# First Wq loads on ScalarE's queue, finished rows on SyncE's or ScalarE's, and a new order of all operations

## The chip, the cores and the metric

The kernel runs on one core of a Trainium2 chip. The metric is the device time of one execution in microseconds (us). The engines are TensorE (PE), VectorE (DVE), ScalarE (ACT), GpSimd (POOL) and SyncE (SP). PE multiplies into PSUM, DVE, ACT and POOL do the elementwise work, and SP issues most transfers. Each engine carries out its own instructions strictly in order and waits, where it has to, on semaphores that the others raise.

## The reference, cut to what matters

A cross-attention layer in fp32: batch 2, 2048 tokens, width 640, 8 heads of 80; the context has 128 tokens, of which the last 4 (`ca`) belong to an adapter.

```python
query = x @ Wq;  keyt = enc @ Wk;  valt = enc @ Wv        # enc: 124 text tokens
hs    = mha(query, keyt, valt)                            # text attention
ca_q1 = einsum('btc,th->bch', ca, Wq_ca)[:, indices, :]   # 384 rows, each repeated for 2048 positions
ca_hs1 = mha(ca_q1, x, x)                                 # adapter, first attention: over all tokens
ca_hs2 = mha(ca_hs1 @ Wq, ca @ Wk_ca, ca @ Wv_ca)         # adapter, second attention: 4 keys
out = (hs + ca_hs2) @ Wout + b_out + x
```

## The kernel before, in words

All text work goes through 16 units of 256 tokens, 8 for each of the two samples. For each unit PE makes queries (`pq`, out of transposed rows `xt` and `wq_sb`), scores against the text keys (`sc`), attention outputs (`ph`, out of transposed probabilities `pT`) and the output projection (`po`). Queries and projection are products with fewer multiplications: sums and differences of blocks go in (`x_sums`, `wq_sums`, `wout_sums`, and for each `ph` a set of sums in `hs`), partial products go through PSUM and are added by DVE (`q`, and the two buffers of output rows, `x_more` and `last_rows`). A row tile starts as a load of x, gathers its projections by adds on DVE and the adapter's part by an accumulating indirect transfer of POOL (`add_second`: `x_more<-o,query` or `last_rows<-o,query`), and is stored to `out_dram`.

The adapter runs beside it, sample by sample. Its first scores are made twice. The first time (`s<-zop,cop`) DVE only takes their maxima (`mx`, 128 x 2048 elements at a time, 24 for each sample); the second time ACT takes exponentials (`ea`, again 24 for each sample), and PE sums them against `y_sb` into `acc`. A tile of first scores gets its bank of PSUM only when DVE has read the one before it. From `acc` a short chain (`prod`, `s2f`, `p`, then the transpose `pt_p` on PE, `p2T`, `po`, `o`) makes the second attention's result `o`, which `add_second` gathers from DRAM.

The order of everything is written out by hand, or rather by a search whose result is a table. Coroutines give operations (`Do`: engine or engines, function, what it waits for). The class `Desk` (L64) has a table `TURNS` (L85 to L292) with a number for each operation. `Desk.run` takes the operation with the lowest number, and the number modulo six names the engine. So the table alone sets each engine's order and, where a `Do` names several engines, which of them does the work. `Desk.dma` (L445) puts a transfer on ACT's queue when the table gave it to ACT, otherwise on SP's; its times (`us`, `issue`, `more`) are only the search's idea of a transfer, and don't reach the program. Transfers of both queues share eight completion semaphores, in turn: a transfer waits at its issue until the one eight places ahead of it, on either queue, has landed.

At the start, 14 `unread` products of zeros keep PE busy ahead of and between its first real work, and `first_loads` (L667) loads four row tiles of x (`xz`) and Wq (`wq_sb`) in five pieces, all on SP in the order x0, Wq0, x1, Wq1, Wq2, Wq3, the five strips of Wq4, x2, x3, `wqca`, the context, and two more weights. `residual` (L2329) loads rows, `stored` (L2507) stores them: POOL accumulates, then SP stores. The last unit's rows go out in halves (`stored_half`, L2498), on SP or ACT.

Of the kernel before, what the change touches and what calls it, by code (L numbers as in the profile page):

```python
# [14 lines left out]
P = 128  # L15
# [50 lines left out]
class Desk:  # L66
# [393 lines left out]
def kernel(  # L460
# [206 lines left out]
    def first_loads():  # L667

        def whole(at):
            t = xrow.tile([P, 4 * H], F32, tag="xz", name="xz")  # L670
            rows_of[0] = t.rearrange("p (k n) -> p k n", k=4)

        yield Do("NONE", whole, [], needs=[(staging, 1)])

        def x_rows(k):
# [26 lines left out]
        for c in (2, 3):  # L702
            yield chunk(c)
# [1887 lines left out]
```

## Time and profile before

| | us |
|---|---|
| Median of 3 runs (573.73, 575.43, 575.57) | 575.43 |
| The profiled execution, its own time | 576.6 |
| Its span, first to last instruction | 574.9 |
| PE busy | 564.9 (98%) |
| DVE busy | 399.1 (69%) |
| ACT busy | 285.4 (50%) |
| POOL busy | 167.3 (29%) |
| Mean granted TensorE clock | 0.996 |

The profiled execution lies 1.2 us above the median and 1.7 us of it lie outside the span. PE is busy for all but 10 us of the span, so a new order can win little more than those: 1.1 us ahead of PE's first instruction, some 3.3 us behind its last, and short waits between. The engines' shares are means over stages with different limits. In one stage DVE takes the maxima and is itself busy without a gap; in another ACT takes the exponentials; in the last 75 us only PE has much to do, and POOL and the transfers of rows run beside it. What a wait costs has to be read in its stage.

### The profile page before, as it was taken

The page shows a single profiled execution, that of the slowest core. Times are in us where ns is not written, and L with a number is a line of the kernel's source. Part 1 is how long each engine was busy: PE and PEld are TensorE (multiplying, and loading weights), DVE is VectorE, ACT ScalarE, POOL GpSimd, SP SyncE. Part 2 cuts the span into 40 slices and gives each one's busy share as a digit, 9 for nine tenths or more (in the row PEclk, how much of TensorE's full clock was granted, in tenths as well). Part 3 has the DMA queues.
Part 4 walks back from the last instruction along what each step waited for, and adds up shares of the span by engine and source line. Part 5 has one row for each costly group of instructions (what it writes and reads, how often), then busy time and mean ns, then how long its engine had stood idle before and what let it go on. Part 6 is the DMA issues. An engine that isn't in the chain of part 4 may idle for free.

```text
span 574.9 us, 18865 instructions
## 1 busy us (share of the span) xinstructions
PE 564.9 (98%) x8069; PEld 307.9 (54%) x8069; DVE 399.1 (69%) x657; ACT 285.4 (50%) x808; POOL 167.3 (29%) x220
## 2 busy tenths in 40 slices
PE   9999999999999999999989999999999999999987
PEld 8885334555556455465545454555545545455543
DVE  2475999999998656567999999996422332645353
ACT  1113255476656799899845556534646664000000
POOL 8202023310622062103114342521412141155162
PEclk9999999999999999999989999999999999999999
DMA  7998485876878867536725989886564496889978
GB/s 221 219 245 137 142 174 156 158 203 146 199 193 192 233 161 185 163 122 188 249 65 166 315 247 324 210 268 227 140 207 93 138 271 196 247 201 240 261 132 244
DMA packets 145690, 113.20 MB, mean 197 GB/s; under 512 B 82548, under 2 KB 116980, under 8 KB 145608
## 3 DMA queue, kind: packets, MB, share of 16 engines
q1 hardware_dynamic: 139688, 101.00, 61.1%
q0 software_dynamic: 5632, 10.69, 10.8%
q8 instruction: 63, 1.03, 0.7%
q10 hardware_dynamic: 288, 0.33, 0.2%
q14 instruction: 19, 0.16, 0.1%
HBM read 71.60 MB, written 40.39 MB: 195 GB/s over the span
## 4 chain that ended last, share of the span: by engine, by line
PE 85%; DVE 6%; DMA 4%; ACT 4%; issue 1%; POOL 0%; SPq 0%; ACTq 0%; POOLq 0%
PE po L405 24%; PE pq L405 21%; PE acc L396 7%; PE sc L396 7%; PE s L396 6%; PE ph L396 6%; PE pq L396 4%; PE pyz L396 2%; DVE mx L427 2%; ACT ea L427 2%; DMA out_dram<-x_more 2%; DMA last_rows<-o,query 1%; PE pv L396 1%; PE pk L396 1%; ACT p L427 1%
## 5 line engine op out<-in xcount | busy, mean ns | idle before, releaser
L427 ACT ACTIVATE p<-sc,m 128x124 f32<-128x124 f32 x256 | 90.1, 379 | 42.8 <-DVE m L427 42.8
L427 DVE TENSOR_REDUCE mx<-s 128x4 f32<-128x2048 f32 x48 | 109.2, 2275 | 1.3 <-PE s L396 1.2
L427 ACT ACTIVATE ea<-s 128x2048 f32<-128x2048 f32 x48 | 90.7, 1890 | 35.9 <-PE s L396 35.8
L427 POOL TENSOR_TENSOR p<-p,r 128x992 f32<-128x992 f32 x16 | 30.2, 1891 | 176.9 <-DVE r L427 175.4
L405 PE MATMUL po<-wout_sums,hs 128*32 128x320 f32 x1024 | 78.4, 434 | 1.6 <-POOL hs L427 1.6
L405 PE MATMUL po<-wout_sb,hs 128*32 128x320 f32 x928 | 71.5, 433 | 0.1
L405 PE MATMUL pq<-xt,wq_sb 128*32 128x256 f32 (+1 forms) x928 | 66.6, 422 | 0.0
L427 DVE TENSOR_TENSOR x_more<-x_more,po 128x320 f32<-128x320 f32 x68 | 32.3, 480 | 43.4 <-PE po L405 42.9
L427 DVE TENSOR_TENSOR last_rows<-last_rows,po 128x320 f32<-128x320 f32 x60 | 28.4, 482 | 41.4 <-PE po L405 41.2
L427 ACT ACTIVATION_READ_ACCUMULATOR p<-sc,m 128x1 f32 x256 | 56.6, 221 | 0.0
L427 POOL TENSOR_TENSOR hs<-hs 128x256 f32<-128x256 f32 x35 | 32.5, 953 | 63.6 <-DVE hs L427 56.3
L405 PEld LDWEIGHTS po<-wout_sums,hs 128*32 128x32 f32 x1024 | 31.7, 110 | 35.8 <-issue 3.2
L396 PE MATMUL acc<-ea,y_sb 128*32 128x384 f32 (+2 forms) x768 | 50.2, 383 | 0.4 <-ACT ea L427 0.4
L396 PE MATMUL ph<-pT,vpad 128*32 128x256 f32 x768 | 47.5, 380 | 0.0
L427 DVE TENSOR_REDUCE m<-sc 128x4 f32<-128x496 f32 x64 | 40.5, 659 | 9.1 <-PE sc L396 9.0
L2350 POOL DMA_INDIRECT x_more<-o,query x17 | 26.7, 1571 | 64.6 <-DVE x_more L427 34.5
L405 PEld LDWEIGHTS po<-wout_sb,hs 128*32 128x32 f32 x928 | 29.3, 110 | 30.1 <-issue 1.2
L405 PEld LDWEIGHTS pq<-xt,wq_sb 128*32 128x32 f32 x928 | 28.3, 111 | 28.9 <-issue 14.6
L427 DVE STREAM_TRANSPOSE eb<-p 128x1024 f32<-128x1024 f32 x32 | 39.4, 1233 | 2.5 <-DMA kept<-eb 1.4
L396 PEld LDWEIGHTS sc<-kmain,q 64*128 64x128 f32 x512 | 31.5, 187 | 12.2 <-issue 6.1
L396 PE MATMUL sc<-kmain,q 64*128 64x124 f32 x512 | 37.6, 284 | 0.0
L405 PE MATMUL pq<-xt,wq 128*32 128x512 f32 x280 | 34.1, 595 | 0.0
(219 smaller groups left out, 823.3 us busy)
## 6 DMA issues: line engine op xcount, KB each, us to landing
kept<-eb SPq DMA_DIRECT2D x32, 512.0 KB, 4.2
pT<-kept SPq DMA_DIRECT2D x16, 1024.0 KB, 7.6
landing<-away SPq DMA_DIRECT2D x15, 512.0 KB, 4.7
xi<-in_x_dram SPq DMA_DIRECT2D x56, 128.0 KB, 4.0
x_more<-in_x_dram SPq DMA_DIRECT2D x17, 320.0 KB, 4.5
out_dram<-x_more SPq DMA_DIRECT2D x16, 320.0 KB, 5.1
last_rows<-in_x_dram SPq DMA_DIRECT2D x15, 320.0 KB, 6.5
out_dram<-last_rows SPq DMA_DIRECT2D x14, 320.0 KB, 3.7
```

Of the source, the lines that this page charges most:

```text
L396: self.pin(self.nc.tensor.matmul(out, lhsT, rhs, **kw))
L405: self.pin(self.nc.tensor.matmul(out[j : j + 32], lhsT[:, j : j + 32], rhs, **kw))
L427: self.pin(getattr(engine, what)(*args, **kw))
L2350: desk.pin(nc.gpsimd.indirect_dma_start(out=t, out_offset=None, in_=o2_of[b], in_offset=bass.IndirectOffsetOnAxis(ap=query[:, st : st + 1] ...
```

## The change

Three things. The loads of Wq become a task of their own on ACT's queue, so that SP issues the four row tiles one behind the other. `stored` may use SP or ACT, and the table chooses: in the changed program 14 finished row tiles or halves are stored by ACT, where before only the last two halves were. And the whole table is new; it was searched with other numbers for how long transfers take (the third arguments and `more` of the calls of `dma`), which themselves leave the program as it is. PE's work is the same in both programs: 4494 products, the 14 of zeros among them.

```diff
     TURNS = {
-        ".1": [791], ".2": [38, 53, 54, 72, 84, 96, 102, 114, 126, 156, 168, 180, 192, 198, 234, 762], ".3": [536],
+        ".1": [1025], ".2": [44, 59, 60, 84, 96, 108, 114, 120, 126, 132, 150, 174, 198, 210, 234, 1002], ".3":
...
+        def of_wq():
+
+            for c in range(4):
+                yield chunk(c)
+            yield Do("ACT", last, [], marks=[("wq", 4)])
+
...
-            return Do("SP", go, [], marks=[("wq", c)])
+            return Do("ACT", go, [], marks=[("wq", c)])
...
-        for k in (0, 1):
-            yield x_rows(k)
-            yield chunk(k)
-        for c in (2, 3):
-            yield chunk(c)
-        yield Do("SP", last, [], marks=[("wq", 4)])
-        for k in (2, 3):
+        yield Fork(of_wq(), 0)
+        for k in range(4):
             yield x_rows(k)
...
-            "SP", lambda: dma(pT.rearrange("p i k h a -> p i (k h a)"), by_keys, 2.85, 0.42, 2.6),
+            "SP", lambda: dma(pT.rearrange("p i k h a -> p i (k h a)"), by_keys, 3.6, 0.42, 1.9),
...
-        yield Do("SP", lambda: dma(rows_out, t, 0.8, 0.37), frees=[(rows, i)])
+        yield Do(("SP", "ACT"), lambda: dma(rows_out, t, 1.15, 0.37, 1.45), frees=[(rows, i)])
...
-        desk.free[e] = 0.8
+        desk.free[e] = 0.85 if e == "ACT" else 0.8
```

The places that the prediction speaks of follow, as each engine's order stands in the two programs. The numbers behind names are those of buffers.

DVE at the second attention of sample 0, before: `m`, `p` and `r` are its small softmax, `mx` the maxima of the first scores of sample 1, `eb` and `q` belong to the text units.

```order
L427 TENSOR_REDUCE m_0_3849<-s2f 128x24
L427 TENSOR_TENSOR p_0_3705<-s2f,m_0_3849 128x96
L427 TENSOR_REDUCE mx_3252<-s_1_0_1_0_3838 128x4
L427 STREAM_TRANSPOSE eb_1_3899<-p_831 128x1024
L427 TENSOR_REDUCE r_0_3706<-p_0_3705 128x24
L427 RECIPROCAL r_0_3706<-r_0_3706 128x24
L427 TENSOR_TENSOR p_0_3705<-p_0_3705,r_0_3706 128x96
L427 TENSOR_TENSOR q_3752<-q_3752,pq_1_3855 128x2x256
L427 TENSOR_TENSOR q_3752<-q_3752,pq_0_3753 128x2x256
```

The same place after.

```order
L427 TENSOR_REDUCE m_0_3833<-s2f 128x24
L427 TENSOR_TENSOR p_0_3699<-s2f,m_0_3833 128x96
L427 RECIPROCAL r_3_3722<-r_3_3722 128x8
L427 TENSOR_REDUCE mx_3167<-s_1_0_1_0_3836 128x4
L427 SCALAR_TENSOR_TENSOR zop_3_3585<-zop_3_3585,low_z,zb_3_0_3724 128x512
L427 STREAM_TRANSPOSE eb_1_3897<-p_830 128x1024
L427 TENSOR_REDUCE r_0_3700<-p_0_3699 128x24
L427 RECIPROCAL r_0_3700<-r_0_3700 128x24
L427 TENSOR_TENSOR p_0_3699<-p_0_3699,r_0_3700 128x96
L427 TENSOR_TENSOR q_3752<-q_3752,pq_0_3753 128x2x256
L427 TENSOR_TENSOR q_3752<-q_3752,pq_1_3861 128x2x256
```

The combination of `zop`, which before stood ahead of `prod`, `s2f` and `m`, now stands behind the maxima, and the two adds into `q` have changed places. In both programs the transpose `pt_p` on PE waits for the add that reads `pq_1`.

POOL in the last 75 us, before: `hs` are sums of a unit's attention outputs, the DMAs accumulate the adapter's rows.

```order
L427 TENSOR_TENSOR hs_5056<-hs_5056 128x256
L2350 DMA last_rows<-o_1_6406,query 128x640
L427 TENSOR_TENSOR hs_4223<-hs_4223 128x256
L2350 DMA x_more<-o_1_6406,query 128x640 x2
L2350 DMA last_rows<-o_1_6406,query 128x640
L427 TENSOR_TENSOR hs_5056<-hs_5056 128x256
L2350 DMA x_more<-o_1_6406,query 128x640
L427 TENSOR_TENSOR hs_4130<-hs_4130 128x256
L2350 DMA x_more<-o_1_6406,query 128x640 x2
L2350 DMA last_rows<-o_1_6406,query 128x640 x3
```

The same after.

```order
L427 TENSOR_TENSOR hs_5064<-hs_5064 128x256
L2351 DMA last_rows<-o_1_6388,query 128x640
L2351 DMA x_more<-o_1_6388,query 128x640
L427 TENSOR_TENSOR hs_5064<-hs_5064 128x256 x2
L2351 DMA x_more<-o_1_6388,query 128x640 x4
L2351 DMA last_rows<-o_1_6388,query 128x640
L427 TENSOR_TENSOR hs_5064<-hs_5064 128x256
L2351 DMA x_more<-o_1_6388,query 128x640
L2351 DMA last_rows<-o_1_6388,query 128x640 x3
```

Before, the third `hs` sum here is the first of the four sums of its unit that the projection needs. After, that sum is DVE's, made right behind its copy of `ph`; POOL's last `hs` sum is the one that the projection needs last.

ACT among the exponentials of sample 1, after; before, this stretch of ACT held the same exponentials and copies and no DMA.

```order
L427 ACTIVATE ea_1_7_6082<-s_1_1_7_6073 128x2048
L427 COPY hs_5064<-ph_2_6094 128x512
L447 DMA out_dram<-last_rows 128x640
L427 ACTIVATE ea_1_8_6124<-s_1_1_8_6115 128x2048
L447 DMA out_dram<-x_more 128x640
L447 DMA out_dram<-last_rows 128x640
L427 COPY wout_sums<-ph_4_6125 128x256
L427 ACTIVATE ea_1_9_6178<-s_1_1_9_6169 128x2048
L427 ACTIVATE ea_1_10_6213<-s_1_1_10_6204 128x2048
```

SP's last transfers, before; the last two half rows of all are ACT's.

```order
L447 DMA out_dram<-x_more 128x640 x2
L447 DMA out_dram<-last_rows 128x320
L447 DMA out_dram<-last_rows 128x640
L447 DMA out_dram<-x_more 128x640
L447 DMA out_dram<-last_rows 128x640
L447 DMA out_dram<-last_rows 128x320
L447 DMA out_dram<-last_rows 128x640
```

SP's last transfers after; ACT stores the first half of the very last row, SP the second, and a whole row behind it.

```order
L447 DMA out_dram<-x_more 128x640
L447 DMA last_rows<-in_x_dram 128x640
L447 DMA x_more<-in_x_dram 128x640
L447 DMA out_dram<-x_more 128x640
L447 DMA out_dram<-last_rows 128x640 x2
L447 DMA out_dram<-x_more 128x320 x2
L447 DMA out_dram<-last_rows 128x640
```

More of the change, by code (lines that the diff above doesn't have):

```diff
@@ L676, in x_rows @@
             return Do(
-                "SP", lambda: dma(rows_of[0][:, k], x[0, k * P : (k + 1) * P, :], (0.3, 0.9, 1.65, 1.65)[k], more=2.3),
+                "SP", lambda: dma(rows_of[0][:, k], x[0, k * P : (k + 1) * P, :], (0.45, 0.9, 1.2, 1.2)[k], more=2.3),
                 [], marks=[("xrows", k)],
@@ L685, in go @@
                 if c < 2:
-                    dma(wq_sb[:, c, :], pair, 1.65, more=2.3)
+                    dma(wq_sb[:, c, :], pair, (0.45, 1.0)[c], more=2.3)
                 else:
@@ L1360, in of_pairs @@
                 d1 = VR + (R * i + VH) % P
-                dma(most[part, :2], v[:, 0::2, :, d0 : d0 + R], 2.16, 1.31)
+                dma(most[part, :2], v[:, 0::2, :, d0 : d0 + R], 1.7, 1.31)
                 desk.pin(nc.sync.dma_start(most[part, 2:], v[:, 1::2, :, d1 : d1 + R]))
@@ L1708, in part_away @@
             def part_away(i, k=k, z=z):
-                dma(away[k, :, i].rearrange("q (g n) -> q g n", g=4), z[:, i].bitcast(F32), 0.31, 0.45)
+                dma(away[k, :, i].rearrange("q (g n) -> q g n", g=4), z[:, i].bitcast(F32), 0.48, 0.45, 1.6)
             op = yield Do("ACT", lambda: desk.a_copy(z[:, 0], pq[:, cols]), [at], rank=0)
@@ L1797, in yz_block @@
                 yield Do(
-                    "SP", lambda u=u: dma(away[:, u], zs, 0.65, 0.38), frees=[(zss, i)],
+                    "SP", lambda u=u: dma(away[:, u], zs, 0.3, 0.38, 1.8), frees=[(zss, i)],
                     marks=[("zop", b, sb, u, "away")],
@@ L1811, in back @@
                     zs = cap.tile([P, 512], F32, tag=f"zs{z[0]}", name=f"zb_{b}_{sb}_{u}")
-                    dma(zs, away[:, u], 1.2, 0.38)
+                    dma(zs, away[:, u], 1.15, 0.38, 1.4)
                     return zs
@@ L1847, in away @@
             def away(t=op.value, u=u):
-                dma(kept[:, :, u, :], t.rearrange("p (a n) -> p a n", a=4), 0.85, 0.53)
+                dma(kept[:, :, u, :], t.rearrange("p (a n) -> p a n", a=4), 0.9, 0.53, 1.6)
             yield Do("SP", away, frees=[(yts, op.slots[0][0])], marks=[("y out", b, sb, u)], rank=0.5)
@@ L1862, in back @@
                     y_sb[R * a : R * (a + 1), sb].rearrange("p g u s k -> p g (u s k)"),
-                    by_tokens[a], 0.59, 0.38,
+                    by_tokens[a], 0.67, 0.38, 1.7,
                 )
@@ L2108, in second @@
                 yield Fork(one(Do(
-                    "SP", lambda ct=ct: dma(o2_of[b][ct * P : (ct + 1) * P, :], o2[:, ct], 1.2, 0.37),
+                    "SP", lambda ct=ct: dma(o2_of[b][ct * P : (ct + 1) * P, :], o2[:, ct], 0.9, 0.37, 1.75),
                     [("o2 part", b, ct)], marks=[("o2 out", b, ct)],
@@ L2335, in load @@
                 t = row_of[at[0]]
-                dma(t, x[b, st * P : (st + 1) * P, :], 0.95, 0.37)
+                dma(t, x[b, st * P : (st + 1) * P, :], 1.06, 0.37, 1.85)
                 return t
```

410 rows, old and new, of the table TURNS are left out of this document.

## The prediction

> **What bounds the kernel now.** I read the busy shares of the page first, then all that PE waited for, then a table of stages, and then the instructions at each wait.
>
> ```profile
> PE 564.9 (98%) x8069; PEld 307.9 (54%) x8069; DVE 399.1 (69%) x657; ACT 285.4 (50%) x808; POOL 167.3 (29%) x220
> ```
>
> PE is the bound: of a span of 574.9 us it is idle for 10.0. Its waits, grouped by what ended them (total, times, longest, in us):
>
> ```profile
> PE s L396 <- DVE mx L427: 2.1, 4, 1.1
> PE po L405 <- POOL hs L427: 1.6, 1, 1.6
> PE unread L396 <- DVE zeros L427: 1.1, 1, 1.1
> PE s L396 <- ACT ea L427: 0.6, 3, 0.2
> PE pt_p L396 <- DVE q L427: 0.5, 1, 0.5
> PE acc L396 <- ACT ea L427: 0.4, 2, 0.2
> ```
>
> Two places hold most of what an order can change: the maxima with the second attention's `pt_p` (2.1 + 0.5), and one `po` that waits for POOL (1.6). The stages (from:to, length; busy of PE, PEld, DVE, ACT, POOL; granted clock; share of the DMA engines; GB/s):
>
> ```profile
> 7.17:20.00 12.83, 12.81 (x77) 11.54 (x77) 5.64 (x19) 2.31 (x6) 9.49 (x18) 1.00 0.89 274
> 290.00:300.00 10.00, 8.26 (x116) 4.61 (x108) 9.24 (x12) 3.15 (x12) 0.00 (x0) 0.83 0.25 79
> 293.90:297.30 3.40, 2.97 (x36) 1.57 (x40) 3.40 (x4) 0.60 (x2) 0.00 (x0) 0.50 0.73 231
> 300.00:390.00 90.00, 88.99 (x1280) 46.51 (x1280) 87.03 (x103) 48.13 (x199) 34.45 (x31) 1.00 0.84 254
> 440.00:500.00 60.00, 60.00 (x946) 29.61 (x942) 22.72 (x53) 28.41 (x22) 12.68 (x11) 1.00 0.67 196
> 545.00:556.00 11.00, 9.41 (x144) 4.42 (x140) 6.44 (x14) 0.86 (x2) 7.04 (x6) 1.00 0.62 132
> ```
>
> From 7 us on, PE lacks nothing at the start (12.81 of 12.83). Around 290 us DVE is the bound, 9.24 of 10.00, and stays near it to 390 (87.03 of 90). There the clock is granted at half for 3.40 us, which costs 1.7 us of PE's work beside the waits. Both programs give PE the same products, so the sum is made of waits, the clock, the start and the tail.
>
> **The start.** Moved: Wq's eleven loads go from SP to ACT, two ahead of ACT's table load, the rest between and behind its first three copies of transposes. Before, ten of them held SP:
>
> ```profile
> 2.19 8.24 SPq L447 DMA_DIRECT2D wq_sb<-in_L_xattn_Wq_dram  x10
> 1.13:7.17 6.04, 6.04 (x28) 5.79 (x28) 1.62 (x6) 0.96 (x1) 5.66 (x34) 1.00 0.85 259
> ```
>
> SP was through with them at 10.43, and x2 and x3 came only then. Now the x rows come early, and PE turns row 2 before Wq's second chunk. But PE already had cover for the late rows: it is busy for 6.04 of 6.04 us from its first instruction to 7.17, then for 12.81 of 12.83, and the 14 products of zeros stay. So there is nothing to win, and I put the term at 0. The last strips of Wq now wait on ACT for rows and context to land; PE needs them some 6 us later than SP's last issue of them before, and that cover would have to be used up first. The other end is a loss of 1.0, a little more than the 8.24 / 10 that one of these loads took SP.
>
> **Sample 0's second attention, and the maxima of sample 1.**
>
> ```profile
> 283.84 0.74 DVE L427 SCALAR_TENSOR_TENSOR zop<-zop,low_z,zb 128x512 fp32r<-128x512 f32 x1
> 289.38 2.28 DVE L427 TENSOR_REDUCE mx<-s 128x4 f32<-128x2048 f32 x1
> 293.49 1.28 DVE L427 TENSOR_TENSOR q<-q,pq 128x512 f32<-128x512 f32 x2
> 316.52 0.82 DVE L427 TENSOR_TENSOR wout_sums<-wout_sb 128x640 f32<-128x640 f32 x1
> 291.71 0.51 PE L396 MATMUL s<-zop,cop 32*128 32x512 f32 x4 [1.12 <-DVE mx L427]
> 294.22 1.08 PE L396 MATMUL pt_p<-ident,p 128*32 128x128 f32 x16 [0.52 <-DVE q L427]
> 316.66 0.51 PE L396 MATMUL s<-zop,cop 32*128 32x512 f32 x4 [0.40 <-DVE mx L427]
> ```
>
> `zop` (0.74, some 0.70 net, since neighbours overlap) now follows the maxima at 289.38 instead of preceding them. So the first wait falls from 1.12 to 0.42. But everything DVE does up to `pt_p`'s release is still done, `zop` included, so `pt_p` is released no earlier, and PE stands there 0.70 longer. Worse, `pt_p` waits for the add that reads `pq_1`. It was the first of the pair at 293.49; now it is the second, 1.28 / 2 = 0.64 later. The two waits make 0.42 + (0.52 + 0.70 + 0.64) = 2.28 against 1.64: a loss of 0.64. Further on, one more subtraction, `wout_sums` (0.82), which followed the maxima that end at 316.6, stands ahead of them, and the next `s` is held by that much, less an overlap: up to 0.75. If the two add up, the loss is 1.39, if the second hides in the first, 0.64. I take 1.0. The best end is a gain of 1.1, the 1.12 gone and nothing in its place; the worst, 1.9, adds one more wait like the 0.52, since between 300 and 390 DVE has only 3 us of idle time to give.
>
> **The wait on POOL at 550.9.** The chain of waits, then POOL and PE:
>
> ```profile
> 524.61 7.70 DMA last_rows<-o,query
> 534.41 8.89 DMA out_dram<-x_more
> 543.31 4.92 DMA x_more<-in_x_dram
> 548.34 1.55 POOL L2350 DMA_INDIRECT last_rows<-o,query  x1 [5.67 <-DMA x_more<-in_x_dram]
> 549.33 1.56 POOL L427 TENSOR_TENSOR hs<-hs 128x256 f32<-128x256 f32 x1
> 550.94 1.28 PE L405 MATMUL po<-wout_sums,hs 128*32 128x320 f32 x16 [1.59 <-POOL hs L427]
> ```
>
> SP waits for an accumulate to land before it may store, then for the store to land before it may load the next row; POOL waits for that row; behind it in POOL's order stands the `hs` sum that PE needs. The new order gives this sum to DVE, and POOL's last `hs` sum is used some 8 us of PE's work later. So this wait goes whatever the stores do: -1.59. What is late next is DVE's pair of sums of the same unit, which end close before their use; I leave 0.2 for it. Net -1.4, between -1.6 and 0 (POOL's new place as late as the old).
>
> [...]
>
> **The tail.** Rows of the last 55 us (KB each, median us from issue to landing), and the last issue:
>
> ```profile
> out_dram<-last_rows SPq DMA_DIRECT2D x6, 320.0 KB, 3.6
> out_dram<-x_more ACTq DMA_DIRECT2D x2, 160.0 KB, 1.9
> last_rows<-o,query POOLq DMA_INDIRECT x6, 6.7
> 571.65 0.88 ACTq L447 DMA_DIRECT2D out_dram<-x_more  x2
> ```
>
> Before, a half row on ACT is last. Now SP issues a half when the last add is done and a whole row behind it. That adds one issue, 0.88 / 2 = 0.4, and between nothing and 3.6 - 1.9 = 1.7 for the longer landing. At the very end little else is in flight, so I take 0.4 of this: +0.8, between 0.4 and 2.1.
>
> **The other moves cost nothing** that I can place. The twelve stores that ACT gains besides the two cost it 12 x 0.44 = 5.3 us of issue; it is idle for half of the span (285.4 busy). The `pT` loads keep their places ahead of `ph`.
>
> **The sum**, against the profiled execution's 576.6: 0 + 1.0 - 1.4 + 0.8 = +0.4, so 577.0. That execution lies 1.2 above the median of 575.43, so I say 575.8.
>
> **The rivals.**
>
> Faster: the half clock doesn't come back. It stands at 293.9 to 297.3, behind the waits of 1.12 and 0.52; yet the 1.59 at 550.9 left the clock at 1.00 (545 to 556), so how a wait falls decides, not its length alone. In the new order one wait is short and one long. If the clock stays full and the waits shrink by what I let them grow: 575.8 - 1.7 - 1.0 = 573.1. Against it: the same 2 us of waiting lie in the same 4 us. [...]
>
> Slower: a store on ACT stands ahead of exponentials and waits for its accumulate.
>
> ```profile
> L427 ACT ACTIVATE ea<-s 128x2048 f32<-128x2048 f32 x48 | 90.7, 1890 | 35.9 <-PE s L396 35.8
> SPq L447 <- DMA x_more<-o,query: 41.5, 6, 16.0
> SPq L447 <- DMA last_rows<-o,query: 40.8, 5, 17.4
> ```
>
> On SP such stores waited 82.3 us in 11 times from 440 us on, harmlessly. On ACT, `ea` stands behind, PE's `acc` behind that. An exponential has 35.9 / 48 = 0.75 us of idle time ahead of it, so a store that waits longer delays PE. By the durations of PE's instructions, the closest store among the exponentials stands 6.1 us behind its accumulate, the next 6.7, and an accumulate takes 1.55 on POOL and up to 6.7 to land: waits of 2.2 and 1.6, less 0.75 each, 2.3, and 0.5 for the transfers that then wait for their semaphore's turn. 575.8 + 2.8 = 578.6. Against it: in 440 to 500 PE never waited (60.00 of 60.00), ACT being busy for 28.41, so PE takes the exponentials late.
>
> The move of Wq's loads doesn't do what it says: the strips come late by the 1.0 above, 575.8 + 1.0 = 576.8.
>
> **Chances.** The forecast 0.40 (574.5 to 577.5 by its own terms), the faster rival 0.27, the slower 0.28, the last 0.05. A measurement here tells about 0.3%, 1.7 us, from no change. Faster is the first rival and an edge of the forecast, 0.28; the same is most of the forecast and of the last, 0.38; slower is the second rival with the upper edge, 0.34. The range, 572.2 to 579.0, takes in both rivals' middles.
>
> **What would show it.** Right: no `po` waiting for POOL; `pt_p` waiting near 1.9 us for `q`; a wait at `s` near 316; a whole `last_rows` store landing last, some 3.5 us behind PE's end. Wrong: `acc` waiting for `ea` by more than 0.4 in all, stores on ACT with waits above 0.75 ahead of `ea`, a clock of 1.00 through 290 to 300, or PE idle between 7 and 20 us.

## The result

The changed kernel takes 573.27 us (median of 17 runs, 572.9 to 574.38). The kernel before, run beside it, takes 575.96 us (17 runs, 573.73 to 580.09). The ratio is 0.994, with a 95% interval from 0.992 to 0.996: faster by about 0.6%. The forecast was 575.8, within 0.3% of no change, in a range from 572.2 to 579.0. The time lies in the range, but on the side that had a chance of 0.28.

The runs of the changed kernel lie within 1.5 us of each other, those of the kernel before spread over 6. The profiled execution of the changed kernel took 572.92 us, with a span of 570.9; against the 576.6 and 574.9 of the one before that is 3.7 to 4.0 us, more than the medians' 2.7, because the profiled execution before was slower than its median (by 0.64) and the one after faster (by 0.35). The time falls by 0.3 less than the span: every run of the changed kernel has 2.0 to 2.1 us outside the span, every run of the kernel before 1.7 to 1.8. The prediction had no term for this, and no trace here shows what it is.

### The profile page after: what moved, and what is told of

Read it like the earlier page. It is cut to its first block, busy times and chain, and to the rows that moved or that the text cites. A ratio compares the mean times of both kernels' runs of the same rounds, so it can differ in the third digit from the quotient of the medians.

```text
span 570.9 us, 18875 instructions
## 1 busy us (share of the span) xinstructions
PE 563.0 (99%) x8069; PEld 309.6 (54%) x8069; DVE 394.5 (69%) x659; ACT 287.1 (50%) x806; POOL 160.1 (28%) x213
## 4 chain that ended last, share of the span: by engine, by line
PE 93%; ACT 3%; DVE 3%; DMA 1%; issue 0%; SPq 0%; ACTq 0%
PE po L405 28%; PE pq L405 24%; PE sc L396 8%; PE acc L396 7%; PE ph L396 7%; PE s L396 7%; PE pq L396 4%; PE pyz L396 2%; ACT ea L427 2%; PE pv L396 1%; DVE mx L427 1%; PE pk L396 1%; DMA xz<-in_x_dram 1%; ACT p L427 1%; PE pt_wq L410 1%; PE pw L396 0%
## 5 line engine op out<-in xcount | busy, mean ns | idle before, releaser
L427 POOL TENSOR_TENSOR p<-p,r 128x992 f32<-128x992 f32 x17 | 31.4, 1849 | 130.9 <-DVE r L427 130.9
L405 PEld LDWEIGHTS po<-wout_sums,hs 128*32 128x32 f32 x1024 | 33.4, 110 | 32.7 <-issue 2.7
L427 ACT COPY hs<-ph 128x512 f32<-128x512 f32 (+1 forms) x25 | 13.4, 552 | 57.7 <-PE ph L396 57.7
L427 POOL TENSOR_TENSOR hs<-hs 128x256 f32<-128x256 f32 x31 | 28.9, 1020 | 33.7 <-ACT hs L427 25.4
```

The lines of the kernel that those rows point to most:

```text
L405: self.pin(self.nc.tensor.matmul(out[j : j + 32], lhsT[:, j : j + 32], rhs, **kw))
L427: self.pin(getattr(engine, what)(*args, **kw))
```

## The profile after, beside the one before

The page of the changed kernel, PE's busy time and its waits (total, times, longest):

```profile
PE 563.0 (99%) x8069; PEld 309.6 (54%) x8069; DVE 394.5 (69%) x659; ACT 287.1 (50%) x806; POOL 160.1 (28%) x213
...
PE unread L396 <- DVE zeros L427: 1.1, 1, 1.1
PE s L396 <- DVE mx L427: 1.1, 2, 0.7
PE s L396 <- ACT ea L427: 0.6, 3, 0.2
PE pt_x L410 <- DVE first_rows L427: 0.4, 1, 0.4
PE pt_x L410 <- POOL band_z L541: 0.2, 1, 0.2
PE acc L396 <- ACT ea L427: 0.2, 1, 0.2
```

The wait of 1.6 for POOL's `hs` is gone, and so is that of `pt_p` for `q`. The waits at the maxima are halved. DVE's busy time fell by 4.6 us and POOL's by 7.2.

The stages that answer to the prediction's (from:to, length; busy of PE, PEld, DVE, ACT, POOL; granted clock; share of the DMA engines; GB/s):

```profile
7.17:20.00 12.83, 12.45 (x71) 11.13 (x70) 7.05 (x27) 1.22 (x3) 8.96 (x18) 1.00 0.94 192
290.00:300.00 10.00, 10.00 (x152) 5.87 (x144) 9.93 (x11) 6.94 (x26) 0.00 (x0) 1.00 0.58 196
...
545.00:556.00 11.00, 11.00 (x169) 6.42 (x164) 5.18 (x13) 0.00 (x0) 6.96 (x5) 1.00 0.84 170
```

Between 290 and 300 PE is now busy for all 10.00 us at full clock, where before it was 8.26 at a clock of 0.83.

How far PE is ahead is read from products that both programs have in like number. PE's groups by tile, with the starts of the first and the last product, before:

```profile
L396 PE MATMUL sc<-kmain,q x512: 272/272/371, 71.3 to 389.2; 64*128 64x124 f32 x171
L405 PE MATMUL po<-wout_sums,hs x1024: 429/432/458, 320.2 to 570.1; 128*32 128x320 f32 x171
```

and after:

```profile
L396 PE MATMUL sc<-kmain,q x512: 272/272/371, 71.0 to 385.8; 64*128 64x124 f32 x171
L405 PE MATMUL po<-wout_sums,hs x1024: 429/432/457, 320.1 to 565.2; 128*32 128x320 f32 x171
```

That splits the 4.0 us between the spans by the prediction's terms:

| stretch | forecast | by the traces | read from |
|---|---|---|---|
| start, to the first `sc` | 0 | -0.3 | 71.3 to 71.0 |
| to the last `sc`, with the second attention and the maxima | +1.0 | -3.1 | 389.2 to 385.8, less 0.3 |
| to the last `po`, with the wait on POOL | -1.4 | -1.5 | 570.1 to 565.2, less 3.4 |
| the tail | +0.8 | +0.9 | the spans, less 4.9 |
| sum | +0.4 | -4.0 | |

Three terms came within 0.3. The second is 4.1 off and carries the whole gain. At that place DVE's and POOL's instructions in the timeline of the kernel before (start, us, what):

```profile
284.68 2.28 DVE L427 TENSOR_TENSOR prod<-prod 128x288 f32<-128x288 f32 x2
...
284.84 1.95 POOL L427 TENSOR_TENSOR p<-p,r 128x992 f32<-128x992 f32 x1 [14.97 <-DVE r L427]
...
286.75 1.34 POOL L427 TENSOR_TENSOR x_sums<-xt,x_sums 128x512 f32<-128x512 f32 x1
286.99 1.20 DVE L427 TENSOR_TENSOR s2f<-prod 128x72 f32<-128x72 f32 x1
288.06 1.28 POOL L427 TENSOR_TENSOR x_sums<-xt 128x512 f32<-128x512 f32 x1
...
288.22 0.25 DVE L427 TENSOR_REDUCE m<-s2f 128x24 f32<-128x96 f32 x1
...
288.51 0.95 DVE L427 TENSOR_TENSOR p<-s2f,m 128x96 f32<-128x96 f32 x1
```

and the same DVE instructions after, one by one (shape, busy, mean ns):

```profile
L427 DVE TENSOR_TENSOR prod<-prod 128x144 f32<-128x144 f32 x1 | 0.3, 307 | 0.0
L427 DVE TENSOR_TENSOR p<-s2f,m 128x96 f32<-128x96 f32 x1 | 0.3, 259 | 0.0
L427 DVE TENSOR_REDUCE m<-s2f 128x24 f32<-128x96 f32 x1 | 0.3, 253 | 0.0
L427 DVE TENSOR_TENSOR s2f<-prod 128x72 f32<-128x72 f32 x1 | 0.2, 234 | 0.0
```

Before, the pair of `prod` took 2.28 us, `s2f` 1.20 and `p` 0.95; now 0.76, 0.23 and 0.26, together 3.18 us less, on the same shapes. Before, each of the three ended 0.1 to 0.2 us behind one of POOL's additions and multiplications: 286.96 behind 286.79, 288.19 behind 288.09, 289.46 behind 289.34. The reduction `m`, which reads one operand, took 0.25 in both, beside POOL's 288.06 as well. In the new order none of these POOL instructions stands there: the multiplication of `p` by `r` is ACT's, and of the two `x_sums` one is DVE's and one POOL's, the latter over at 277.6, 6 us ahead of the chain.

## The experiments

The theory after the result was P, for POOL: a DVE instruction with two operands in SBUF is held until a POOL instruction that is under way has ended (the three above end 0.10 to 0.17 us behind POOL's), which before held DVE back by 3.2 us just ahead of the maxima that PE waits for. The rival was O, for order: the gain comes from `zop` behind the maxima, from the other moves of DVE or from the late part. In each edit a number of the table moves one operation, or gives it to another engine (its remainder by six). A line with a minus sign gives the number that stood in the table.

**Before, with POOL's three instructions behind DVE's chain.** POOL's first one waits for a reciprocal of DVE, which here stands behind `p` instead of ahead of `prod`. No engine's work changes.

```diff
-Desk.TURNS[".66.2.2"][6] = 7502
+Desk.TURNS[".66.2.2"][6] = 7538
```

> The kernel before, with one reciprocal of VectorE (0.14 us) moved behind the second attention's chain, so that GpSimd's multiplication and two sums behind it start only after the chain. Theory P (VectorE's elementwise operations with two inputs in SBUF wait for GpSimd's, so prod, s2f and p took 4.4 us instead of 1.3): prod 0.8 for the pair, s2f 0.23, p 0.26, no wait at s near 291 nor at pt_p, no half clock there, 3 to 3.5 us faster than before where that clock was halved, at least 1.6 anyway. Theory O (the gain came from zop standing behind the maxima): prod, s2f and p as long as before, waits 1.1 and 0.5 as before, 0 to 0.3 us.

Measured: 573.35 us (13 runs, 571.71 to 580.07); ratio 0.9932, interval 0.9901 to 0.9962. One reciprocal moved makes the median of the kernel before as low as that of the changed one, though its runs spread over 8.4 us. From the timeline of DVE and POOL:

```profile
284.66 0.76 DVE L427 TENSOR_TENSOR prod<-prod 128x288 f32<-128x288 f32 x2
285.45 0.23 DVE L427 TENSOR_TENSOR s2f<-prod 128x72 f32<-128x72 f32 x1
...
286.00 0.26 DVE L427 TENSOR_TENSOR p<-s2f,m 128x96 f32<-128x96 f32 x1
...
286.52 1.84 POOL L427 TENSOR_TENSOR p<-p,r 128x992 f32<-128x992 f32 x1 [16.61 <-ACT p L427]
...
289.58 1.28 POOL L427 TENSOR_TENSOR x_sums<-xt 128x512 f32<-128x512 f32 x1
...
290.19 0.78 DVE L427 TENSOR_TENSOR p<-p,r 128x96 f32<-128x96 f32 x1
```

The three are short as in the changed kernel. The next one of the kind, the second multiplication of `p`, now meets POOL's last one: 0.78 instead of 0.26, and it ends at 290.97, 0.1 behind POOL's 290.86. That this happens again at another place, with another instruction, speaks for P and leaves next to nothing for O. PE waits neither at `s` near 291 nor at `pt_p`, as expected, but a wait of 0.51 for the maxima is left at a `po` at 294.52. The profiled execution was the slowest of the 13, with a wait of 4.4 us for POOL's `hs` near 551, of which more below.

**Before, with the `hs` sum on DVE.** The one sum that PE waits for at 550.9.

```diff
-Desk.TURNS[".64.3.4"][0] = 13221
+Desk.TURNS[".64.3.4"][0] = 13220
```

> The kernel before, with one hs sum of the last unit but one given to VectorE instead of GpSimd, nothing else. If the wait of 1.59 us near 551 hangs on this sum standing behind an accumulate in GpSimd's order, it goes and the kernel is 1.4 to 1.6 us faster. Rival (the stores on ScalarE's queue are what ends it): another po or ph waits for rows or transfers there, gain below 0.5 us.

Measured: 576.34 us (12 runs, 575.11 to 578.91); ratio 0.9995, interval 0.9966 to 1.0023. The wait is gone, the time is not measurably less; the expected gain of 1.4 to 1.6 isn't seen, though the interval alone, which reaches to 2.0 us, would not exclude it. The trace says where the time went. Stages of this kernel:

```profile
563.00:567.00 4.00, 4.00 (x64) 1.95 (x60) 1.45 (x3) 0.00 (x0) 0.84 (x1) 1.00 1.06 250
567.00:571.00 4.00, 2.69 (x40) 1.04 (x32) 1.48 (x4) 0.00 (x0) 0.00 (x0) 1.00 1.05 342
571.00:575.00 4.00, 0.00 (x0) 0.00 (x0) 0.00 (x0) 0.00 (x0) 0.00 (x0) 0.97 0.53 199
```

PE's last product ends at 569.69, 1.9 earlier than before, but the span ends at 575.0: the tail is 5.3 us, where before it was 3.3. The DMA engines are busy throughout (1.06 and 1.05 of the stretch) and still moving rows when PE is done. In the kernel before, the last two of these stretches read:

```profile
567.00:571.00 4.00, 4.00 (x68) 1.93 (x60) 1.29 (x3) 0.00 (x0) 0.00 (x0) 1.00 0.99 334
571.00:575.00 4.00, 0.61 (x12) 0.02 (x3) 0.97 (x2) 0.00 (x0) 0.00 (x0) 0.85 0.54 201
```

The transfers end when they ended before (0.53 and 0.54 of the last 4 us). So in this order the wait at 551 covered the transfers, and taking it away alone hands its time to the tail. In the same trace the waits near 291 stand as before (1.12 and 0.52), but the clock stayed full there, and instead a third wait of 1.22 came at 296.6. The half clock and that wait are two faces of one lateness of DVE: from the start of the late `s` to the start of the first `po` behind it PE took 5.41 us in the trace with the half clock (291.71 to 297.12), and 5.40 here without it (291.21 to 296.61).

**Both edits together.**

> The kernel before with both edits. If the two waits are all that matters, it reaches the changed kernel's time: 3.0 to 5.0 us faster than before, within 1 us of 573.3, and its times spread as little as the changed kernel's (under 2 us). If the start, the stores on ScalarE or the rest of the new order carry a share, it stays 1 to 2 us above 573.3.

Measured: 573.43 us (12 runs, 571.96 to 578.37); ratio 0.9939, interval 0.9906 to 0.9972: what the first edit gives, and no more. Here too the tail is 5.3 us. The other half of the expectation failed: the runs spread over 6.4 us, where I had expected under 2.

**The changed kernel, with those POOL instructions as before.** The multiplication of `p` goes from ACT to POOL, one `x_sums` from DVE to POOL, and these, the reciprocal ahead of them and POOL's own `x_sums` stand at before's places; everything else stays new.

```diff
-Desk.TURNS[".66.2.2"][6] = 7454
-Desk.TURNS[".66.2.2"][7] = 7609
-Desk.TURNS[".54.4"][0] = 7293
-Desk.TURNS[".54.3"][0] = 7148
+Desk.TURNS[".66.2.2"][6] = 7502
+Desk.TURNS[".66.2.2"][7] = 7539
+Desk.TURNS[".54.4"][0] = 7593
+Desk.TURNS[".54.3"][0] = 7629
```

> The changed kernel with GpSimd's multiplication and two sums put back beside the second attention's chain, as they stood before. Theory P: prod, s2f and p take 4 to 4.5 us again, s and pt_p wait 1.5 to 2.5 us together, and the half clock may come back: 1.5 to 4 us slower than the changed kernel, 574.8 to 577.3. Theory O: prod, s2f and p stay at 1.3 us and the time within 0.5 us of 573.3.

Measured: 577.0 us (12 runs, 576.54 to 577.48); ratio 0.9992, interval 0.9962 to 1.0022. The whole gain is gone. DVE's groups, then the stage, PE's scores by tile, and PE's waits in the timeline:

```profile
L427 DVE TENSOR_TENSOR prod<-prod 128x144 f32<-128x144 f32 x1 | 1.8, 1833 | 0.0
L427 DVE TENSOR_TENSOR s2f<-prod 128x72 f32<-128x72 f32 x1 | 1.2, 1195 | 0.0
L427 DVE TENSOR_TENSOR p<-s2f,m 128x96 f32<-128x96 f32 x1 | 0.9, 945 | 0.0
```

```profile
290.00:300.00 10.00, 8.24 (x104) 4.73 (x100) 9.31 (x14) 4.54 (x15) 0.00 (x0) 0.83 0.30 93
```

```profile
L396 PE MATMUL sc<-kmain,q x512: 272/272/371, 71.0 to 389.6; 64*128 64x124 f32 x171
```

```profile
290.67 0.51 PE L396 MATMUL s<-zop,cop 32*128 32x512 f32 x4 [0.46 <-DVE mx L427]
...
294.44 1.08 PE L396 MATMUL pt_p<-ident,p 128*32 128x128 f32 x16 [1.28 <-DVE q L427]
```

The long instructions are back, to within 5 ns of before's, the last `sc` comes 3.8 later than in the changed kernel, and the waits have the shape that I had forecast: a short one at `s` (0.46; I had 0.42), a longer one at `pt_p` (1.28; I had 1.86), and the half clock. The second is shorter than forecast because PE took 0.50 us more for the scores between them (2.49 against 1.99 before). From the moment PE was free for this `s` to the start of `pt_p` it took 4.23 us, and 3.63 before: 0.60 more, where I had 0.64. My reading of the order of DVE was right for a kernel in which POOL is still there.

**The changed kernel, all stores of finished rows on SP.** Twelve of the fourteen stores that ACT issued go back to SP; the last two halves were ACT's before, too. One line of the twelve:

```diff
+Desk.TURNS[".58.3.10"][2] = 10096
...
```

> The changed kernel with all twelve of its stores of finished rows that had gone to ACT's queue back on SP's, in before's manner; everything else stays. Theory P (the whole gain lies in the stretch 286 to 300, where POOL no longer holds DVE up, and the wait at 551 went because its sum is on DVE): within 0.5 us of the changed kernel's 573.3, no `po` waiting for POOL's `hs`, PE busy 11.00 of 11.00 in 541 to 552; SP waits longer for the accumulates. Theory S (the stores on ACT are what makes the late part smooth): a wait of PE for POOL or for a last sum comes back past 500, 574.5 to 576, and the runs spread as before's do.

Measured: 573.36 us (8 runs, 573.23 to 574.39); ratio 0.9942, interval 0.9919 to 0.9964: the changed kernel's time. PE waits for no POOL sum there, and waits 0.3 us less in all. The queue of the stores is worth nothing here: 573.36 against 573.27.

**The changed kernel, the first loads of Wq on SP.** Four chunks and the five strips go between the rows of x again. The two lines that name the engine, beside nine numbers of the table:

```diff
-            yield Do("ACT", last, [], marks=[("wq", 4)])
+            yield Do("SP", last, [], marks=[("wq", 4)])
...
-            return Do("ACT", go, [], marks=[("wq", c)])
+            return Do("SP", go, [], marks=[("wq", c)])
```

> The changed kernel with the first loads of Wq back on SP's queue, between the rows of x, as before. My term for their move was 0 (between 0 and a loss of 1.0). Theory 0: 573.3 within 0.4, PE's idle time ahead of 20 us moves by less than 0.4. Rival G (the move gains, by rows that come earlier): 573.9 to 574.5, PE waits for rows 2 and 3. Rival L (the move costs, as its two waits of 0.23 and 0.38 us at 4.8 and 8.0 suggest): 572.7, those two waits gone.

Measured: 575.77 us (12 runs, 574.88 to 577.77); ratio 0.9969, interval 0.9946 to 0.9993. That is 2.4 more than the run with the stores on SP beside it, more than either rival gave. Its waits at the start:

```profile
PE pt_x L410 <- DMA xz<-in_x_dram: 0.7, 2, 0.4
PE pt_x L410 <- DVE first_rows L427: 0.7, 1, 0.7
```

PE is 1.36 us behind the changed kernel when these are over, at 13.3 us, and keeps that distance to 317. Another 1.35 come in five steps of 0.2 to 0.4 between 317 and 515, most of it where the trace shows no wait of PE (one holds a wait of 0.18 for ACT); what makes them I can't say. So the new order of PE's first products needs the rows early, and the move pays for that. Against the kernel before it wins next to nothing: the run with both edits above, with its loads of Wq on SP in before's order, starts its first `sc` at 70.7, the changed kernel at 71.0.

**The changed kernel, the whole row stored ahead of the last half.**

```diff
-Desk.TURNS[".64.3.9"][2] = 13684
+Desk.TURNS[".64.3.9"][2] = 13672
```

> The changed kernel with one change in the order of SP's queue at the very end: the whole row is stored ahead of the last half row and no longer behind it. My term for this was a loss of 0.8 that the changed kernel's trace shows as 0.85 (4.15 us between PE's end and the span's against 3.3). If the term is right: 572.5, some 3.4 us behind PE's end. Rival: the last half's landing then takes the place of the row's, and the time stays at 573.3.

Measured: 573.02 us (7 runs, 572.56 to 573.42); ratio 0.9924, interval 0.9895 to 0.9954. In the trace the tail is 3.43 us instead of 4.15, as expected, but PE's last product ends 0.6 later, by three steps between 450 and 515, of which a wait for ACT explains 0.17. Of 0.7 expected the median shows 0.25, within what runs differ by: inconclusive.

**The same, and `wout_sums` behind the maxima.** One of these is DVE's subtraction, whose wait I had put at up to 0.75; the other is a subtraction of POOL that the new place pushes back (the expectation calls both DVE's).

```diff
-Desk.TURNS[".76.1"][0] = 8150
-Desk.TURNS[".76.3"][0] = 8199
+Desk.TURNS[".76.1"][0] = 8228
+Desk.TURNS[".76.3"][0] = 8235
```

> As the run with the tail put back, and besides DVE's two `wout_sums` subtractions behind the maxima of their units instead of ahead of them: the two waits at `s` for `mx` (0.45 at 309.6, 0.66 at 313.3 in the changed kernel) should shrink to 0.1 to 0.4 in all. If waits of the trace add up: 571.7 to 572.0. Rival: what DVE doesn't do there it does later, the wait comes back at the next `s` or at a `po` that uses `wout_sums`, and the time is that of the run with the tail alone, 572.5.

Measured: 577.28 us (12 runs, 575.65 to 578.91); ratio 1.0004, interval 0.9983 to 1.0026. Neither expectation: 4 us lost. POOL's timeline, and PE's:

```profile
313.80 3.19 POOL L427 TENSOR_TENSOR wout_sums<-wout_sb,wout_sums 128x640 f32<-128x640 f32 x2 [8.75 <-DVE wout_sums L427]
316.95 3.02 POOL L427 TENSOR_TENSOR hs<-hs 128x256 f32<-128x256 f32 x4
```

```profile
319.33 1.82 PE L405 MATMUL po<-wout_sb,hs 128*32 128x320 f32 x24 [2.95 <-POOL hs L427]
```

POOL's two `wout_sums` wait for DVE's, and POOL's four `hs` sums, which PE needs next, stand behind them in POOL's order. The maxima's second wait fell by 0.2, and PE lost 2.95 at that `po`.

**The same again, POOL's `hs` sums ahead of its `wout_sums`.**

```diff
+Desk.TURNS[".56.3.5"][0] = 8253
+Desk.TURNS[".56.3.6"][0] = 8259
+Desk.TURNS[".56.3.7"][0] = 8265
+Desk.TURNS[".56.3.4"][0] = 8277
-Desk.TURNS[".76.3"][0] = 8235
-Desk.TURNS[".76.4"][0] = 8271
+Desk.TURNS[".76.3"][0] = 8295
+Desk.TURNS[".76.4"][0] = 8319
```

> The run that put DVE's two `wout_sums` behind the maxima lost 3 us at one `po`, because POOL's two `wout_sums` wait for DVE's and POOL's four `hs` sums stand behind them. Here the same move on DVE, but POOL's `hs` sums stand ahead of its `wout_sums`; the tail as in the run with the whole row first. Theory Q (the loss was POOL's order alone): no wait of `po` for POOL, 572.8 to 573.0, at most 0.2 under the run with the tail, since only 0.2 of the waits for the maxima went. Rival: the POOL sums are also slowed by DVE's own additions beside them, and a wait above 0.5 stays: 573.5 or more.

Measured: 572.53 us (12 runs, 572.25 to 573.75); ratio 0.9941, interval 0.9917 to 0.9966. POOL's timeline:

```profile
311.36 3.63 POOL L427 TENSOR_TENSOR hs<-hs 128x256 f32<-128x256 f32 x4 [6.32 <-ACT hs L427]
314.95 3.19 POOL L427 TENSOR_TENSOR wout_sums<-wout_sb,wout_sums 128x640 f32<-128x640 f32 x2
```

No `po` waits. This is 0.3 under what Q gave (572.8 to 573.0), so Q's cause is right and its size is not shown. It has the lowest median of all kernels here, 0.7 below that of the changed kernel in the same comparison; the runs of the two overlap.

**Both kernels once more.**

> The changed kernel itself once more, beside the others on the same chip. If its gain is in its order and not in the luck of one execution: 573.3 within 0.4, runs within 2 us of each other, clock 1.00 from 286 to 300, no wait of PE for POOL's `hs`.

> The kernel before, profiled once more. The wait at the maxima near 291 and DVE's long instructions beside POOL's stand in its order and should come again (1.1 and 0.5 us; products 2.3 us for two). The first 30 us (0.7 us between executions so far) and the `po` that waits for POOL near 551 (1.59 in one, 4.39 in a run with the same order there) hang on when transfers land and should differ.

The changed kernel took 573.24 us (12 runs, 572.88 to 573.8) against 575.8 for the kernel before (23 runs, 573.76 to 579.94): ratio 0.9953, interval 0.9932 to 0.9974. In its trace the waits are the same but for the start, 0.47 in one piece. The one execution of the kernel before took 579.56. In its timeline and stages:

```profile
292.60 0.50 PE L396 MATMUL s<-zop,cop 32*128 32x512 f32 x4 [1.12 <-DVE mx L427]
...
295.11 0.64 PE L396 MATMUL pt_p<-ident,p 128*32 128x128 f32 x16 [0.52 <-DVE q L427]
...
298.00 0.82 PE L396 MATMUL po<-w_sb,p2T 32*128 32x320 f32 x8 [1.22 <-DVE mx L427]
```

```profile
290.00:300.00 10.00, 7.13 (x120) 4.20 (x116) 9.32 (x12) 2.84 (x8) 0.23 (x1) 1.00 0.25 80
545.00:560.00 15.00, 12.99 (x176) 5.94 (x172) 6.86 (x15) 0.86 (x2) 7.73 (x7) 0.89 0.64 130
```

As expected, the first two waits came again to 0.01 us and DVE's long instructions to 0.02. The half clock didn't come; in its stead PE waits 1.22 at a third place, and comes out of the stretch at the same distance (within 0.1 us of the first trace's). The wait for POOL near 551 was 2.0 here, 1.6 in the first trace, 4.4 in the run with the moved reciprocal, and with the two long ones came a lower clock (0.89 here and 0.77 in that run between 545 and 560, 1.00 in the first trace). These, and the start, move from one execution to the next, and the changed kernel has no such wait. They don't explain the narrow spread of its runs, though. The kernel before with both edits has neither the waits near 291 nor the one near 551 in its trace, and its runs spread over 6.4 us; the changed kernel with POOL's work back has half clock and long waits, and its runs spread over 0.9. What makes the spread stays open.

## Why the prediction was right or wrong

**The start** (0, between 0 and a loss of 1.0): right in size, but not for the reason given. The first `sc` starts at 71.0 in both traces of the changed kernel, and at 70.7 to 71.3 in the five traces with before's start, so the -0.3 of the table is no more than executions differ by. I had argued that PE's cover stays; but one of my signs of being wrong came, PE idle for 0.38 us between 7 and 20 us, and putting the loads back costs 1.36. The zero is a balance of the move and of the new order of PE's first products, which I hadn't seen: luck, in part.

**The second attention and the maxima** (+1.0): wrong, -3.1, and this is the step that failed. I said that "everything DVE does up to `pt_p`'s release is still done", "so `pt_p` is released no earlier", and so took the time that DVE's work ahead of it had before as its price. Three durations in it, those of `prod`, `s2f` and `p` (2.28, 1.20 and 0.95), which the prediction doesn't even show, were 3.18 us too long together (the three take 1.25 in the changed kernel), because POOL worked beside them; the order of POOL at this place changes, and I looked only at DVE's. The trace of before alone would have told: 0.95 us for `p` at 288.51, and 0.26 at 293.31 for the next instruction of this shape:

```profile
293.31 0.26 DVE L427 TENSOR_TENSOR p<-p,r 128x96 f32<-128x96 f32 x1
```

That the lengthening comes from POOL is shown from both sides, by the moved reciprocal (573.35 against 576.98) and by POOL's three instructions put back (0.9992 of the kernel before, where the changed kernel is 0.994). The traces show it instruction by instruction: the lengthened two-operand ones of this chain end 0.1 to 0.2 us behind POOL's, the first of the `prod` pair, which began ahead of POOL's multiplication (284.68 against 284.84), took 0.41 and wasn't lengthened (0.45 in the changed kernel), and the reduction with one operand took 0.25 beside POOL and without it.

Within this term the order of `zop` and of the two adds behaves as I had worked out, as the run with POOL's work back shows: there the stretch to the last `sc` is 0.7 us longer than before (71.0 to 389.6 against 71.3 to 389.2), where I had 1.0. `wout_sums` ahead of the maxima came as a wait, but a smaller one: 1.1 us at 309.6 and 313.3, where before there were 0.7 at 313.3 and 316.7. Of these 0.4, moving it back wins 0.2, all of it at the second place, and only if POOL's order moves with it. Ahead of the first place POOL holds DVE up in the changed kernel, too:

```profile
303.62 2.00 DVE L427 SCALAR_TENSOR_TENSOR zop<-zop,low_z,zb 128x512 fp32r<-128x512 f32 x1
...
303.52 1.55 POOL L427 TENSOR_TENSOR wout_sums<-wout_sb 128x640 f32<-128x640 f32 x1 [0.63 <-PE pq L405]
```

This `zop` took 0.74 at 287.37 in the same trace, and here it ends 0.55 behind POOL's `wout_sums` (305.62 against 305.07). DVE has no gap from here to the end of the maxima that PE waits for at 309.6. Whether that is what makes the wait of 0.45 there no run here tests.

**The half clock** (assumed to stay): it went, and I counted it wrongly either way. It isn't a price on top of DVE's lateness. Before, PE lost the same time there with it and without it, as half clock in one trace, as a wait of 1.22 in two others (5.41 us from `s` to `po` with the one, 5.40 with the other). In the changed kernel, with DVE 3.2 us earlier, there was nothing to wait for.

**The wait on POOL** (-1.4): right for this order, -1.5 with what lies between. But it was right only together with the order of the transfers behind it. In the old order the same move of the same sum changed the time by nothing that could be measured (0.9995), the tail taking 2.0 in the trace.

**The tail** (+0.8): right, +0.9. SP's whole row is issued at 567.71 and lands at 569.95, 3.2 us behind PE's end; I had said 3.5.

**The rivals.** The faster one gave 573.1, and the median is 573.27, but its reason, a clock that stays full by the chance of when a wait falls, is not what happened: the waits that it needed weren't there. The slower one, a store on ACT ahead of exponentials, isn't there: PE's `acc` waits 0.2 us for `ea`, and the stores put back on SP changed nothing. The strips of Wq on ACT weren't late.

## What to carry to other kernels

Before a duration from a trace is used as the price of an instruction, compare it with the same shape elsewhere; if it is long, look at what the other engine does in the same microsecond, since a change that moves this other engine changes the price (here by 3.18 us). When an instruction is moved off the critical path, follow whoever waits for its result and what stands behind that on its engine (a subtraction on DVE cost 3 us through POOL's queue). A wait that disappears ahead of a stretch bound by transfers isn't won until the transfers come earlier too (the 1.59 us at 550.9 went, the tail grew from 3.3 to 5.3, and the ratio was 0.9995).

## What the runs showed of the hardware

A DVE instruction of 0.23 to 0.31 us took 0.78 to 1.83 beside POOL's additions and multiplication of 1.28 to 1.95, and each ended 0.1 to 0.2 us behind one of these; POOL's own multiplication was hardly longer (1.95 against the 1.84 that it took beside DVE's maxima in the run with the moved reciprocal). The changed kernel's trace has more of it: an `hs` sum of DVE, 0.38 us at its shortest, took 1.66 at 396.06 and ended 0.28 behind a multiplication of POOL. Copies with one operand aren't free of it, as the reduction was: two of `first_rows`, 0.18 and 0.29 us at the shortest of their shapes, began at 6.19 and 6.30 and took 1.49 and 1.52, ending 0.05 and 0.18 us behind the last of three memsets of POOL.

The granted clock fell to half for 3.40 us after waits of 1.12 and 0.52 in one execution, and stayed full through 1.12, 0.52 and 1.22 at the same place of the same program in another. What decides between the two no trace here shows. What half clock costs is no fixed addition to a sum: where PE is held by another engine anyway, it cost nothing here (5.41 us from `s` to `po` with it, 5.40 without).
